# Maxima by half blocks, and eight weighing-only steps moved among the last groups of a graph attention kernel

## The chip, the core and the metric

The kernel runs on one core of a Trainium2 chip. The core has five engines with queues of their own: TensorE (PE; its weight loads are listed as PEld), VectorE (DVE), ScalarE (ACT), GpSimd (POOL) and SyncE (SP, which here only issues DMAs). The metric is the device time of one execution in microseconds; less is better. The median of several runs stands for a kernel.

## The reference

One layer of relational graph attention with residual and two layer norms, on 3125 nodes of 128 values and 100,000 edges, sorted by destination (about 32 edges to a node), each with one of 5 relations; 8 heads of 16.

```python
x_src, x_dst = node_embeddings[src], node_embeddings[dst]
for r in range(5):
    mask = edge_types == r
    q = jnp.einsum('eh,khd->ekd', x_dst, W_Q[r])
    k = jnp.einsum('eh,khd->ekd', x_src, W_K[r])
    v = jnp.einsum('eh,khd->ekd', x_src, W_V[r])
    logits = (q * k).sum(-1) / 4 + attn_bias[r][None, :]
    masked = jnp.where(mask[:, None], logits, -1e9)
    max_v = jax.ops.segment_max(masked, dst, num_segments=n)
    exp_l = jnp.where(mask[:, None], jnp.exp(masked - max_v[dst]), 0.0)
    sum_exp = jax.ops.segment_sum(exp_l, dst, num_segments=n)
    attn = exp_l / (sum_exp[dst] + 1e-12)
    out = out + jax.ops.segment_sum(attn[:, :, None] * v, dst, num_segments=n)
h = out.reshape(n, 128) @ out_proj_w.T + out_proj_b + node_embeddings
y = layernorm(h) * gamma + beta
result = layernorm(x + y)
```

So every edge needs the largest logit of its node, relation and head before its weight can be formed.

## The kernel before, in words

Edges are cut into 196 groups of 512 in the order of their destinations; nodes into 25 blocks of 128. A first phase (to about 135 us) makes a table `kv_d` of keys and values, one row for each node and relation, the first queries, and the place `start_i` in the edge list where each node begins, with its number of edges `deg`. `checks` counts nodes that have too many edges or begin too far from where an even spread would put them; if there is any, a general path is run in place of this one.

Then comes one loop over steps `k`, written out by hand: the order in which instructions are issued is the order on each engine. A step does the first half of the work for one group `g` and the second half for an earlier group `v`.

First half, group `g`: POOL gathers the group's 512 rows of `kv_d` with four indirect DMAs (`gather`, L618) into one of 24 buffers, in the loop up to three steps ahead (`AHEAD`, one step near the end). SP fetches `kt` (keys for the one-hot matrix `hot`) and `qw` (queries of the nodes in the group's window, L720) three steps ahead. PE spreads the queries over the edges (`spread_q`, L734), DVE multiplies and sums (`logits`, L747, L748), SP stores the logits with their relation to `lg_d` (L753).

Maxima, for each block `b` of 128 nodes, one node on a partition: when the last group that can hold an edge of the block has its logits (`full_at`, step `full_step[b]`), POOL loads 64 edges' logits for each node from `start_i` on (`maxima_load`, tile `ell`, L760). This load stands in POOL's queue behind the gathers issued so far and ahead of all later ones, and it waits for the stored logits. `maxima(b, c0, c1)` then runs in two steps, relations 0 to 2 and 3 to 4: ACT turns `ell` to head-major order (`by_head`, L772), DVE closes the edges of other relations (`shut`, L782), adds (L787) and reduces (L793), on 8 heads x 64 edges for each relation; six small operations split the result into three bfloat16 parts `m3`. SP stores them to `m_d` (`store_m`, L807) and fetches the rows of a window for each later group (`fetch_m`, tile `mw`, L815).

Second half, group `v`: PE spreads the maxima over the edges (`spread_m`, L825), DVE subtracts (`less_max`, L833), ACT takes the exponential (L837), DVE weighs the values (`weigh`, L842), ACT makes the one-hot matrix of places `at` (L862, L865; near the end DVE makes two of its four parts, L857), PE sums by node and relation (`sums`, L876; what belongs to a node cut by the group's edge is carried over, L878), DVE divides (`norm`, L897 to L900), PE adds the relations (L885), and ACT puts the result in its place (`by_node`, L910). A gather's buffer comes free when its group has been weighed.

For each block, when its groups are summed (`done_at`): projection (L917, L918), residual and moments (`residual`), square root on ACT (`roots`, L943, which needs another activation table than the exponential; a table load takes 1.28 us) and norms on DVE (`norms`, L948 to L968), store (L976). A block whose `root_at` would fall between the last group's first half and the last group's second half is put off to the end, so that the table is exchanged once.

The plan: `step_of[g]` is the step of the first half, `at_k[v]` that of the second half. `ready[b] = full_step[b] + lag(b)`, with a lag of 8 steps (7 for the last three blocks): load at `full_step + 1`, maxima at `ready - 5` and `ready - 4`, store at `ready - 3`, fetch from `ready - 2` on. Group `v` may not be weighed before `ready` of the block in which its last node can lie (`block_of`). `CATCH_UP` is a set of groups after each of which a step without a first half is put in; before, it is empty. So the first halves take steps 0 to 195, second halves lag 19 steps in the steady part, and 19 steps (196 to 214) hold only second halves: these are called weighing-only steps here. In them `spread_m` repeats its columns 16 times rather than 8 (only the first copy is used).

Of the kernel before, what the change touches and what calls it, by code (L numbers as in the profile page):

```python
# [17 lines left out]
P = 128  # L18
# [29 lines left out]
CATCH_UP = ()  # L48
# [6 lines left out]
LAG = 8  # L55
SR = 250
# [43 lines left out]
def slack(b):  # L100

    n = min(P * b, N)
    e = E * n / N
    return int(5.0 * max(e * (1 - e / E), 0.0) ** 0.5) + 16 if 0 < n < N else 0


def full_at(b, more=0):

    last = P * E // N * (b + 1) + slack(b + 1) + more
    return -(-min(E, last) // GE) - 1 if b < NT - 1 else NGR - 1  # L110


def block_of(g):

    return min(
        b for b in range(NT)
        if b == NT - 1 or P * E // N * (b + 1) - slack(b + 1) >= min(E, (g + 1) * GE)
    )


def windowed_path(
# [25 lines left out]
    start_i = keep("start_i", [P, NT], I32)  # L147
    deg = keep("deg", [P, NT])
# [126 lines left out]
    cap = load.tile([P, NT], F32, name="cap")  # L275
    for b in range(NT):
        nc.gpsimd.memset(off[:, b : b + 1], float(slack(b)))
        nc.gpsimd.memset(cap[:, b : b + 1], float((full_at(b, D) + 1) * GE - D))
# [194 lines left out]
    begin = load.tile([P, NT + 1], F32, name="begin")  # L473

    def starts():
# [5 lines left out]
        nc.vector.tensor_tensor(start_i, begin[:, :NT], cap, op=ALU.min)  # L481
# [3 lines left out]
        nc.vector.tensor_tensor(deg, endp, begin[:, :NT], op=ALU.subtract)  # L485

    def checks():
        many = load.tile([P, NT], F32, name="many")
        nc.vector.tensor_scalar(
            many, deg, float(D), None, op0=ALU.is_gt, op1=ALU.add, accum_out=vio[:, 3:4]  # L490
# [5 lines left out]
        nc.vector.tensor_tensor(dev[:, 0, :], dev[:, 0, :], off, op=ALU.is_gt)  # L496
        dsum = load.tile([1, 1], F32, name="dsum")
# [17 lines left out]
    def small():  # L515
        nc.vector.tensor_scalar_mul(bias4, bias4, 4.0)
        nc.vector.tensor_tensor(lift, lift, beta_t[0:1, :], op=ALU.subtract)
        op_ = pps.tile([P, P], F32, name="op_", tag="tr", bufs=2)
        nc.tensor.transpose(op_, ow, ident)
        nc.scalar.copy(out_wT, op_)  # L520
# [20 lines left out]
    def no_maxima():  # L541
# [26 lines left out]
        21: [checks],  # L568
# [189 lines left out]
    def maxima_load(b):  # L758
# [3 lines left out]
            in_=lg_d[: (full_at(b, D) + 1) * GE, :],  # L762
# [4 lines left out]
    def maxima(b, c0, c1):  # L767

        if c0 == 0:
            ell = live.pop(("ell", b))  # L770
            by_head = ps.tile([P, HEADS, D], F32, name="by_head", bufs=1)
            nc.scalar.copy(by_head, ell[:, :, :HEADS].rearrange("p s k -> p k s"))  # L772
# [4 lines left out]
            mx = late_flow.tile([P, R, HEADS], F32, name="mx", bufs=1)  # L777
            live["max", b] = by_head, mine, mx
        by_head, mine, mx = live["max", b]
        shut = late_flow.tile([P, RH, D], F32, name="shut", bufs=1)  # L780
        for r in range(c0, c1):
# [3 lines left out]
        wl = late_flow.tile([P, RH, HEADS, D], F32, name="wl", tag="wl", bufs=1)  # L785
        n = c1 - c0
        nc.vector.tensor_tensor(  # L787
            wl[:, :n],
            by_head[:, None].to_broadcast([P, n, HEADS, D]),
            shut[:, :n, None, :].to_broadcast([P, n, HEADS, D]),  # L790
            op=ALU.add,
        )
        nc.vector.tensor_reduce(mx[:, c0:c1], wl[:, :n], AX.X, ALU.max)  # L793
# [3 lines left out]
        nc.vector.tensor_tensor(mx, mx, bias4, op=ALU.add)  # L797
        nc.vector.scalar_tensor_tensor(mx, mx, NEG4, bias4, op0=ALU.max, op1=ALU.subtract)
        m3 = late_flow.tile([P, R, 3, HEADS], BF16, name="m3")
        nc.vector.tensor_copy(m3[:, :, 0, :], mx)  # L800
        nc.vector.tensor_tensor(mx, mx, m3[:, :, 0, :], op=ALU.subtract)
        nc.vector.tensor_copy(m3[:, :, 1, :], mx)
        nc.vector.tensor_tensor(m3[:, :, 2, :], mx, m3[:, :, 1, :], op=ALU.subtract)
        live["m3", b] = m3

    def store_m(b):
        nc.sync.dma_start(  # L807
            m_d[b * P * R : (b + 1) * P * R, :].rearrange("(p r) c -> p (r c)", r=R),
            live.pop(("m3", b)).rearrange("p r s k -> p (r s k)"),
        )  # L810

    def fetch_m(g):
        mw = late_flow.tile([P, 3, HEADS], BF16, name="mw", bufs=4)
        f = window(g, first5, SPE)
        nc.sync.dma_start(mw.rearrange("w s k -> w (s k)"), m_d[bass.ds(f, P), :])  # L815
        live["mw", g] = mw


    def spread_m(g, times):

        me = ps.tile([P, T, times, HEADS], F32, name="me", tag="me")
        hot, mw = live.pop(("hot", g)), live.pop(("mw", g))
        for t in range(T):
            for s in range(3):
                nc.tensor.matmul(  # L825
                    me[:, t], hot[:, t, :], mw[:WR, s, None, :].to_broadcast([WR, times, HEADS]),
                    start=(s == 0), stop=(s == 2),
                )
        live["mde", g] = me[:, :, 0, :]
# [156 lines left out]
    def lag(b):  # L986

        return LAG if b < NT - 3 else LAG - 1

    full_step = [step_of[full_at(b, D)] for b in range(NT)]  # L990
    ready = [full_step[b] + lag(b) for b in range(NT)]


    at_k, k = {}, 0
    for v in range(NGR):
        k = max(k + 1, ready[block_of(v)])
        at_k[v] = k
    v_at = {k: v for v, k in at_k.items()}
    last_k = at_k[NGR - 1]
    done_at = {b: at_k[full_at(b)] + 4 for b in range(NT)}  # L1000
# [26 lines left out]
    for k in range(-3, root_at[NT] + 2):  # L1027
# [8 lines left out]
        for b in range(NT):  # L1036
            if done_at[b] - 1 == k:
                fetch_x("xr", b)
            if norm_at[b + 1] + 1 == k:
                store_z(b)  # L1040
            if ready[b] - 3 == k:
# [3 lines left out]
        for u in range(NGR):  # L1045
            if max(at_k[u] - 3, ready[block_of(u)] - 2) == k:
# [8 lines left out]
        for b in range(NT):  # L1055
# [21 lines left out]
        if v_at.get(k + 1) is not None:  # L1077
            spread_m(v_at[k + 1], 8 if k + 1 in group_at else 16)
# [27 lines left out]
        for b in range(NT):  # L1106
            if ready[b] - 5 == k:
                maxima(b, 0, RH)
            if ready[b] - 4 == k:
                maxima(b, RH, R)  # L1110
# [525 lines left out]
```

## Time and profile before

| | |
|---|---|
| median of 9 runs | 1763.12 us (1741.0 to 1767.3) |
| profiled execution | 1753.77 us, its span 1751.8 us |
| granted TensorE clock, mean | 0.708 |
| busy: PE, PEld | 1022.2 us (58%), 771.9 us (44%) |
| busy: DVE, ACT, POOL | 947.6 (54%), 638.6 (36%), 797.9 us (46%) |
| first logits (L747) | 135.3 us |
| logits of groups 157, 192, 195 | 1386.6, 1655.9, 1673.9 us |
| weighing (L842) of groups 0, 183, 195 | 289.8, 1700.7, 1729.3 us |

Times inside an execution are counted from its first instruction. In a profile line of a timeline there stand start, duration, engine, line, operation, output and inputs with partitions x elements, how many, and in brackets how long the engine had been idle and what ended that. "issue" means that nothing in the profile explains the wait; "remote" that the releaser isn't known.

### The profile page before, as it was taken

What the parts mean: (1) busy time and instruction counts of PE and PEld (TensorE: products, weight loads), DVE (VectorE), ACT (ScalarE), POOL (GpSimd) and SP (SyncE); (2) the same over time, 40 slices, a digit from 0 to 9 for tenths busy, and PEclk for the clock granted to TensorE, in tenths of its full rate; (3) what the DMA queues carried; (4) which work ended last, traced back from release to release, by engine and by line L of the source; (5) the groups of instructions that cost most, each with busy time, mean ns of one, the idle gap of its engine ahead of it and who ended that gap; (6) DMA issues with size and microseconds to landing.
All of it is one profiled execution on the core that took longest, in us unless ns stands there. A gap on an engine that the chain in (4) does not pass through costs nothing.

```text
span 1751.8 us, 26103 instructions
## 1 busy us (share of the span) xinstructions
PE 1022.2 (58%) x7738; PEld 771.9 (44%) x7738; DVE 947.6 (54%) x2531; ACT 638.6 (36%) x2257; POOL 797.9 (46%) x904
## 2 busy tenths in 40 slices
PE   5773727256556646645664575566557556454776
PEld 2442525145345435534453454445345345343664
DVE  2551526265546655754565466556546546553786
ACT  0540103134334434433443353343335334342544
POOL 5507051634535555544545545454454544644300
PEclk7996867577666766866676666766677666666788
DMA  5764243344445445534544444454454444434310
GB/s 132 252 266 125 69 120 69 100 110 114 110 113 128 124 104 134 134 99 111 136 119 108 132 117 116 115 136 108 103 138 111 108 120 107 126 109 104 86 25 14
DMA packets 181508, 203.67 MB, mean 116 GB/s; under 512 B 83508, under 2 KB 146381, under 8 KB 181238
## 3 DMA queue, kind: packets, MB, share of 16 engines
q0 software_dynamic: 40672, 112.08, 22.4%
q1 hardware_dynamic: 136928, 86.33, 20.6%
q10 hardware_dynamic: 3758, 3.51, 0.8%
q8 instruction: 64, 1.05, 0.2%
q14 instruction: 86, 0.70, 0.1%
HBM read 166.51 MB, written 35.29 MB: 115 GB/s over the span
## 4 chain that ended last, share of the span: by engine, by line
DVE 28%; PE 25%; another core or an unknown queue 21%; issue 15%; ACT 6%; DMA 3%; SPq 1%; DVEq 0%; POOL 0%; ACTq 0%; POOLq 0%
PE pp L876 7%; PE me L825 4%; DVE wl L787 4%; DVE mx L793 4%; DVE prod L747 4%; PE qe L734 3%; DVE lg L748 3%; DVE wv L842 2%; PE pr L362 2%; ACT at L862 2%; PE pp L878 2%; DVE hot L725 2%; PE pk L701 1%; PE prq L644 1%
## 5 line engine op out<-in xcount | busy, mean ns | idle before, releaser
L618 POOL DMA_INDIRECT kv<-kv_d,idx x764 | 722.8, 946 | 537.9 <-DVE den L897 278.9
L876 PE MATMUL pp<-wv,at 128*125 128x136 f32 x1568 | 383.1, 373 | 92.6 <-issue 85.1
L876 PEld LDWEIGHTS pp<-wv,at 128*125 128x125 f32 x1568 | 285.8, 246 | 181.9 <-issue 167.0
L734 PE MATMUL qe<-qw,hot 125*128 125x128 bf16 x2352 | 230.6, 254 | 162.3 <-issue 127.6
L825 PE MATMUL me<-mw,hot 125*128 125x64 bf16 (+1 forms) x2352 | 146.4, 216 | 224.6 <-issue 120.8
L734 PEld LDWEIGHTS <-hot 125*128 125x128 bf16 x2352 | 198.3, 123 | 179.4 <-issue 148.9
L862 ACT ACTIVATE at<-row_at,nkey 128x125 f32<-128x125 f32 x744 | 237.6, 398 | 0.0
L825 PEld LDWEIGHTS <-hot 125*128 125x128 bf16 x2352 | 125.2, 112 | 250.4 <-issue 190.6
L833 DVE TENSOR_TENSOR me<-lg,me 128x32 f32<-128x32 f32 x196 | 37.6, 192 | 359.3 <-remote 267.0
L837 ACT ACTIVATE me<-me 128x32 f32<-128x32 f32 x196 | 35.7, 182 | 529.5 <-DVE me L833 447.5
L842 DVE TENSOR_TENSOR wv<-kv,me 128x512 f32<-128x512 f32 x196 | 132.9, 678 | 161.7 <-remote 103.9
L747 DVE TENSOR_TENSOR prod<-kv,qe 128x512 f32<-128x512 f32 x196 | 132.9, 678 | 83.7 <-remote 74.0
L760 POOL DMA_INDIRECT ell<-lg_d,start_i x25 | 23.6, 944 | 308.7 <-ACT me L837 79.0
L878 PE MATMUL pp<-pt,carried 125*5 125x136 f32 x390 | 97.0, 336 | 74.7 <-ACT pt L891 47.8
L748 DVE TENSOR_REDUCE lg<-prod 128x32 f32<-128x512 f32 x196 | 134.5, 686 | 6.8
L910 ACT COPY oT<-pp 128x25 f32 x196 | 33.6, 171 | 273.5 <-PE me L825 90.6
L865 ACT ACTIVATE at<-at 128x500 f32<-128x500 f32 (+1 forms) x196 | 117.3, 599 | 6.2
L644 PE MATMUL prq<-wq,xTq 128*128 128x384 f32 (+1 forms) x88 | 52.0, 687 | 89.1 <-DVE hot L725 72.9
L885 PEld LDWEIGHTS pp<-rsum,o 125*128 125x128 f32 x392 | 80.7, 248 | 16.8 <-issue 16.1
L787 DVE TENSOR_TENSOR wl<-by_head,shut 128x1536 f32<-128x1536 f32 (+1 forms) x50 | 74.5, 1491 | 14.4 <-PE pk L701 6.4
L885 PE MATMUL pp<-rsum,o 125*128 125x25 f32 x392 | 72.6, 265 | 13.2 <-issue 8.7
L793 DVE TENSOR_REDUCE mx<-wl 128x24 f32<-128x1536 f32 (+1 forms) x50 | 74.3, 1487 | 1.7
(182 smaller groups left out, 1179.8 us busy)
## 6 DMA issues: line engine op xcount, KB each, us to landing
kt<-key_d SPq DMA_DIRECT2D x196, 128.0 KB
qw<-q_d SPq DMA_DIRECT2D x196, 96.0 KB
kv_d<-kvs SPq DMA_DIRECT2D x24, 640.0 KB
kv<-kv_d,idx POOLq DMA_INDIRECT x764
q_d<-q SPq DMA_DIRECT2D x22, 480.0 KB
lg_d<-lg SPq DMA_DIRECT2D x196, 18.0 KB
mw<-m_d SPq DMA_DIRECT2D x196, 6.0 KB
xr<-in_x SPq DMA_DIRECT2D x24, 64.0 KB
```

The costliest lines, as they stand in the source:

```text
L618: nc.gpsimd.indirect_dma_start(out=kv[:, t, :], out_offset=None, in_=kv_d[:, :], in_offset=bass.IndirectOffsetOnAxis(ap=idx[:, t, g : g + ...
L734: nc.tensor.matmul(qe[:, t, :], hot[:, t, :], qw[:WR, s, :], start=(s == 0), stop=(s == 2))
L747: nc.vector.tensor_tensor(prod, kv[:, :, :H], live.pop(("qe", g)), op=ALU.mult)
L748: nc.vector.tensor_reduce(lg[:, :, :HEADS], prod.rearrange("p t (k d) -> p t k d", d=HD), AX.X, ALU.add)
L787: nc.vector.tensor_tensor(wl[:, :n], by_head[:, None].to_broadcast([P, n, HEADS, D]), shut[:, :n, None, :].to_broadcast([P, n, HEADS, D]), ...
L793: nc.vector.tensor_reduce(mx[:, c0:c1], wl[:, :n], AX.X, ALU.max)
L825: nc.tensor.matmul(me[:, t], hot[:, t, :], mw[:WR, s, None, :].to_broadcast([WR, times, HEADS]), start=(s == 0), stop=(s == 2),)
L842: nc.vector.tensor_tensor(wv[:, :, :H].rearrange("p t (k d) -> p t k d", d=HD), kv[:, :, H:].rearrange("p t (k d) -> p t k d", d=HD), live ...
L862: nc.scalar.activation(at[:, t, :], row_at[:, :WR], AF.Abs, bias=nkey[:, t, g : g + 1], scale=1.0)
L876: nc.tensor.matmul(pp, at[:, t, :], wv[:, t, :], start=(t == 0), stop=(t == T - 1))
L878: nc.tensor.matmul(pp[:R], carried[:WR, g, :], live.pop(("pt", g - 1)), start=False, stop=False,)
L885: nc.tensor.matmul(op, live.pop(("o5", done)), rsum[:WR], start=True, stop=True)
```

## The change

Three things change together.

1. The last six blocks (19 to 24) have their maxima made by halves of 64 nodes: `MB` now lists 30 parts, 19 whole blocks and 11 halves (the 25th block has 53 nodes, so one half). For a half, the 64 nodes stand on both sets of 64 partitions; the lower set works on heads 0 to 3, the upper on heads 4 to 7. So one pass has 5 relations x 4 heads x 64 edges, and `maxima` runs in one step. Each half has its own `ell` load, `deg` and `start_i` columns (made in the first phase by `halves`), its own `bias_h`, and two stores. `checks` looks at the half-block starts too. The lag is 6 steps for a half (`LAG_H`).
2. `CATCH_UP` gets eight groups: after each of 163, 167, ... 191 a weighing-only step is put in. First halves take steps 0 to 203, second halves end at step 214 as before, and 11 weighing-only steps are left after the last first half. The lag of the second half falls from 19 to 11 steps over the last 33 groups.
3. The layout of `m_d`, `m3` and `mw` is now half the heads, part, head; and a weighing-only step repeats its columns 12 times, not 16.

In the plan blocks 20 and 21 now have their roots at steps 194 and 201; before, both stood behind the last weighing step.

```diff
-CATCH_UP = ()
+CATCH_UP = (163, 167, 171, 175, 179, 183, 187, 191)
...
+LAG_H = 6
+HALVED = 5
...
+NF = NT - 1 - HALVED
+MB = [(P * b, P * (b + 1), None) for b in range(NF)]
+for b in range(NF, NT):
+    MB += [(n, min(n + P // 2, N), b) for n in range(P * b, min(P * (b + 1), N), P // 2)]
+MEND = tuple(n for _, n, _ in MB)
+NM = len(MB)
...
+    def halves():
+
+        hp = pps.tile([P, 2, 2, NT - NF], F32, name="hp", tag="tr", bufs=2)
+        for h in range(2):
+            twice = load.tile([P, 2, P // 2], F32, name=f"twice{h}")
+            nc.vector.tensor_copy(
+                twice, ident[:, None, h * P // 2 : (h + 1) * P // 2].to_broadcast([P, 2, P // 2])
+            )
+            for i, a in enumerate((begin[:, NF:NT], degs[:, NF:])):
+                nc.tensor.matmul(
+                    hp[:, i, h, :], twice.rearrange("p a b -> p (a b)"), a, 
+                    start=h == i == 0, stop=h == i == 1,
+                )
...
         if c0 == 0:
             ell = live.pop(("ell", b))
-            by_head = ps.tile([P, HEADS, D], F32, name="by_head", bufs=1)
-            nc.scalar.copy(by_head, ell[:, :, :HEADS].rearrange("p s k -> p k s"))
+            by_head = ps.tile([P, HEADS, D], F32, name="by_head", bufs=1)[:, :nh]
+            if whole:
+                nc.scalar.copy(by_head, ell[:, :, :HEADS].rearrange("p s k -> p k s"))
+            else:
+                for h in range(2):
+                    at = slice(h * P // 2, (h + 1) * P // 2)
+                    nc.scalar.copy(
+                        by_head[at], ell[at, :, h * nh : (h + 1) * nh].rearrange("p s k -> p k s")
+                    )
...
         nc.vector.tensor_tensor(
-            wl[:, :n],
-            by_head[:, None].to_broadcast([P, n, HEADS, D]),
-            shut[:, :n, None, :].to_broadcast([P, n, HEADS, D]),
+            wl,
+            by_head[:, None].to_broadcast([P, n, nh, D]),
+            shut[:, :n, None, :].to_broadcast([P, n, nh, D]),
             op=ALU.add,
         )
-        nc.vector.tensor_reduce(mx[:, c0:c1], wl[:, :n], AX.X, ALU.max)
+        nc.vector.tensor_reduce(mx[:, c0:c1], wl, AX.X, ALU.max)
...
     def store_m(b):
-        nc.sync.dma_start(
-            m_d[b * P * R : (b + 1) * P * R, :].rearrange("(p r) c -> p (r c)", r=R),
-            live.pop(("m3", b)).rearrange("p r s k -> p (r s k)"),
-        )
+        n0, n1, part = MB[b]
+        m3 = live.pop(("m3", b))
+        to = m_d[n0 * R : (n0 + (P if part is None else P // 2)) * R, :]
+        if part is None:
+            nc.sync.dma_start(
+                to.rearrange("(p r) c -> p (r c)", r=R), m3.rearrange("p r h s k -> p (r h s k)")
+            )
+        else:
+            to = to.rearrange("(p r) (h c) -> h p r c", r=R, h=2)
+            for h in range(2):
+                nc.sync.dma_start(
+                    to[h],
+                    m3[h * P // 2 : (h + 1) * P // 2, :, 0].rearrange("p r s k -> p r (s k)"),
+                )
...
-        return LAG if b < NT - 3 else LAG - 1
+        return LAG if MB[b][2] is None else LAG_H
 
-    full_step = [step_of[full_at(b, D)] for b in range(NT)]
-    ready = [full_step[b] + lag(b) for b in range(NT)]
+    full_step = [step_of[full_at(n, D)] for n in MEND]
+    ready = [full_step[b] + lag(b) for b in range(NM)]
...
-            spread_m(v_at[k + 1], 8 if k + 1 in group_at else 16)
+            spread_m(v_at[k + 1], 8 if k + 1 in group_at else 12)
...
-            if ready[b] - 5 == k:
+        for b in range(NM):
+            whole = MB[b][2] is None
+            if ready[b] - 5 == k and whole:
                 maxima(b, 0, RH)
             if ready[b] - 4 == k:
-                maxima(b, RH, R)
+                maxima(b, RH if whole else 0, R)
```

The last groups of the parts from block 18 on have their logits at steps 153, 157, 161, 166, 171, 176, 181, 185, 190, 195, 200 and 203; before, those of blocks 18 to 24 at 153, 161, 169, 177, 184, 192 and 195. Weighing-only steps stand at 164, 169, 174, 179, 184, 189, 194, 199 and 204 to 214.

## The prediction

> **What bounds the kernel now.** I read the share of each engine first (PE 58%, DVE 54%, POOL 46%: none is full), then the waits of POOL between the logits of group 163 and the last logits, since there the stretch that the change rewrites lies.
>
> ```profile
> POOL kv L618 <- DVE den L897: 40.8, 9, 10.2
> POOL ell L760 <- ACT lg L741: 26.8, 2, 13.4
> POOL ell L760 <- DMA lg_d<-lg: 14.4, 1, 14.4
> POOL ell L760 <- DMA mw<-m_d: 13.6, 1, 13.6
> ```
>
> Columns: total us, times, longest. POOL waits for kv buffers to come free (weighing holds them) and 13.4 to 14.4 us at each load of `ell`, because that load needs the logits of its block's last group and POOL has by then gathered three steps ahead. After it POOL runs without a pause (timeline of POOL, one gather each 1.25 us: 0.95 and 0.30 idle):
>
> ```profile
> 1483.87 0.95 POOL L760 DMA_INDIRECT ell<-lg_d,start_i  x1 [13.40 <-ACT lg L741]
> 1485.12 0.95 POOL L618 DMA_INDIRECT kv<-kv_d,idx  x1 [0.30 <-issue]
> ...
> 1498.88 0.94 POOL L618 DMA_INDIRECT kv<-kv_d,idx  x1 [0.30 <-issue]
> 1503.44 0.94 POOL L618 DMA_INDIRECT kv<-kv_d,idx  x1 [3.62 <-DVE den L897]
> ```
>
> In such a burst the other engines almost stop. Same place, stretches of a window query (us, then busy time of PE, PEld, DVE, ACT, POOL, granted clock, DMA share, GB/s), and the logits on DVE:
>
> ```profile
> 1473.80:1483.80 10.00, 8.13 (x68) 6.53 (x66) 7.87 (x24) 5.30 (x22) 0.00 (x0) 0.59 0.28 47
> 1483.80:1489.00 5.20, 4.25 (x54) 3.45 (x52) 2.32 (x6) 4.74 (x10) 3.92 (x5) 1.00 0.76 220
> 1489.00:1502.50 13.50, 1.63 (x13) 1.09 (x14) 3.72 (x15) 2.19 (x9) 8.38 (x9) 0.62 0.52 137
> ```
>
> ```profile
> 1480.14 0.68 DVE L747 TENSOR_TENSOR prod<-kv,qe 128x512 f32<-128x512 f32 x1
> 1483.81 0.68 DVE L747 TENSOR_TENSOR prod<-kv,qe 128x512 f32<-128x512 f32 x1
> 1493.20 0.20 DVE L833 TENSOR_TENSOR me<-lg,me 128x32 f32<-128x32 f32 x1 [7.05 <-remote]
> 1493.94 0.68 DVE L747 TENSOR_TENSOR prod<-kv,qe 128x512 f32<-128x512 f32 x1
> 1503.82 0.68 DVE L747 TENSOR_TENSOR prod<-kv,qe 128x512 f32<-128x512 f32 x1
> ```
>
> 54 matmuls in the first 5.2 us of the burst, 13 in the next 13.5 us. The step that follows comes 4.0 us after the burst's end (1499.8 to 1503.8). What holds PE back I can't see in these rows (the DMA share is 0.52); I use only that it happens: in the middle of the run too, a burst of 17 (982.5 to 1003.6) lets 52 matmuls through in its first 5.5 us and 17 in the next 15.0. So main steps cost POOL's burst plus what is left of the steps when it has ended, and the kernel is bound by this alternation. At the end it is otherwise: POOL is idle, and the weighing-only steps follow one another.
>
> ```profile
> 1673.90:1700.70 26.80, 19.85 (x151) 16.70 (x149) 24.62 (x78) 11.23 (x46) 0.94 (x1) 0.76 0.09 20
> 1700.70:1729.30 28.60, 28.60 (x294) 23.95 (x292) 22.87 (x91) 19.72 (x85) 0.00 (x0) 1.00 0.04 6
> 1729.30:1751.80 22.50, 6.03 (x36) 4.11 (x35) 12.44 (x54) 4.49 (x15) 0.00 (x0) 0.69 0.08 24
> ```
>
> From the last logits (1673.9) to the first group of the last block weighed (183, at 1700.7): the way through `ell`, maxima, store and fetch. Then 12 more steps of 2.38 us, PE 28.6 of 28.6 busy. Then 22.5 us of projection and norms.
>
> **The end, which gets shorter.** The plan has 227 steps before and after; eight weighing-only steps go from the end into the main part (19 become 11).
> - Six groups (190 to 195) instead of 13 depend on the last part: seven steps fewer at 2.38 = -16.7 us.
> - Maxima of the last part. DVE, by shape:
>
> ```profile
> L787 DVE TENSOR_TENSOR wl<-by_head,shut 128x1536 f32<-128x1536 f32 x25 | 43.9, 1758 | 7.2 <-ACT by_head L772 5.6 <-DVE shut L782 0.7 <-issue 0.3
> L793 DVE TENSOR_REDUCE mx<-wl 128x24 f32<-128x1536 f32 x25 | 43.8, 1753 | 0.9
> L787 DVE TENSOR_TENSOR wl<-by_head,shut 128x1024 f32<-128x1024 f32 x25 | 30.6, 1224 | 7.2 <-PE pk L701 6.4
> L793 DVE TENSOR_REDUCE mx<-wl 128x16 f32<-128x1024 f32 x25 | 30.5, 1220 | 0.9
> ```
>
> A whole block: 1.76 + 1.75 + 1.22 + 1.22, `mine` 0.33, `shut` 0.7, six small ones 1.4 = 8.4 us. A half has 20 x 64 = 1280 elements, midway: 1.49 + 1.49 + 0.33 + 0.7 + 1.4 = 5.4. With the weighing that lay between the two stages (1.7 us), -4.5 on this way; the store is now two DMAs of 24-byte pieces, 0 to +1 us (an estimate: 423 packets of SP's queue around 1006 us took 25 ns each in the mean, and each of 16 engines gets 20 of the 320 pieces): -4.
> - Blocks 20 and 21 are normed in the main part. In the last 22.5 us two of six rounds go, each about 1.7 us (DVE 1738.6 to 1740.4): -3.5, of which the main part pays up to two exchanges of ACT's table, 2 x 2 x 1.28 = 5, if nothing hides them; ACT idles in bursts, I take 0.
> - `times` 12 for 16: 96 for 128 columns in 12 matmuls, 0.83 to 0.67 us, x 6 = -1.
>
> Sum of the end: -16.7 - 4 - 3.5 - 1 = -25 us, bounds -20 and -28.
>
> **The main part, which gets longer.** Logits 157 to 192 take 1386.6 to 1655.9 = 269.3 us before. In POOL's order there now stand, between one `ell` and the next from block 18's load on, 16, 12, 16, 16, 16, 16, 12, 12, 16, 16 gathers where there were 32. Each next `ell` again needs logits that POOL has long passed, and the buffers bind no more, because weighing runs closer behind (19 steps fall to 11): so all gathers between two loads run as one burst. An interval, from logits of the last group of one part to those of the next:
> - logits to `ell`: 1480.1 to 1483.9 = 3.8 us;
> - burst of 17: 17 x 1.25 = 21.2 (of 13: 16.2);
> - burst's end to the third step's main work: 4.0;
> - the fourth and fifth step, one weighing-only. The nearest rows are the two steps after a burst with POOL silent: logits 1473.8, 1480.1, 1483.8 = 6.3 + 3.7; the weighing-only one lacks logits and `qe` (1.4 on DVE): about 8.
>
> So 37 us with 16 gathers; 32 with 12 (185 to 190); 28 with 12 and only four steps (181 to 185); 29 for 157 to 161, which has none alone. Sum: 29 + 4 x 37 + 28 + 32 + 2 x 37 = 311, +42 us. The 5.4 us of half maxima lie under the burst here: `ell` lands 6.3 us after issue (1677.6 to 1683.9) while DVE idles in the crawl. If that cover is gone, each interval gets up to 5.5 more (by_head and chain after the burst).
> Lower bound of an interval: the four steps from 1473.8 to 1503.8 took 30.0 us with a burst of 13; add only a bare weighing step, 2.3: 32.3, the other gathers and maxima hidden. Upper: 30 + 2.3 + 4 x 1.25 + 5.5 = 42.8. I take 37, which is also built from the nearest burst of 17. The last three groups keep their 18 us.
>
> The other queues that the moved steps pass: on SP a weighing-only step issues one `mw` fetch (0.34 us and a register load of 0.27), and eleven halves store twice where six blocks stored once, 16 more x 0.35 = 5.6 us over 311. Behind a store that waits for `m3` stand `kt` and `qw` of three steps ahead, so it takes from that lead first: 0. On ACT a half's two copies (64 partitions x 256 each) cost between 2 x 0.28 (the 136-element copy) and 1.06 (the whole one): under the burst as well.
>
> The PE clock decides part of the 8 us. A weighing-only step's PE work takes 0.83 + 0.91 + 0.40 + 0.50 + 0.30 = 2.9 us at clock 1.00 (step at 1722.2) and 1.44 + 1.67 + 0.62 + 0.82 + 0.46 = 5.0 at half (step at 1673.8). The Trainium skill, "TensorE: Matmul & The Clock Gate", section "What's actually happening", says the array falls to half rate after an idle window of about 3.4 us and needs as long a busy one to come back; it speaks against weighing steps placed behind bursts, and the granted 0.59 in the stretch above agrees. By it the 8 us stand; by the end's row at full clock they would be 6, the sum 16 us less.
>
> Early work: the new small operations in the table phase (`halves`, more `checks`, 11 POOL memsets of 0.23) are about 3 us on DVE and 2.5 on POOL, under the table matmuls: 0, at most +3. The strided `mw` reads have as many columns: 0.
>
> **Sum.** +42 - 25 = +17 on the span 1751.8 (execution 1753.77). The median of the runs, 1763.12, lies 9.4 us above that execution; I put the difference on the median: 1780, and 1782 with half of the early work and table exchanges.
>
> **Rivals.**
> 1. Hidden: alone steps, extra loads and half maxima fit into POOL's 13-us waits. Intervals at 32.3, the three short ones at 27, 25 and 27 (157 to 161 took 26.9 before): 6 x 32.3 + 79 = 273, +4; less 25 = -21: 1742. For it: none of the engines is full. Against: in those waits the steps run that POOL waits for.
> 2. Slower yet: maxima fall behind the burst, as they did for block 22 (burst of 21 from 1592, the next less-max only at 1620.4, then maxima). They then delay the fetch of `mw`, on which the less-max ahead of the next logits waits. Intervals 42.8 (37.8, 33.8, 34): 34 + 6 x 42.8 + 33.8 + 37.8 = 362, +93 - 25 = +68: 1831. It decides from intervals of 40 on. For it: the store now comes two steps after the load. Against: in bursts of 13 two steps still got through.
> 3. The start checks (now at half blocks too) reject the input and the general path runs: over twice the time. Same slack rule as before, so 1%.
>
> **How the numbers follow.** Likeliest (37 us intervals, own range 1762 to 1805) 0.50; hidden 0.27; slower yet 0.22; general path 0.01. Break-even is an interval of some 35 (17 us over nine intervals are 1.9 each). The range takes both rivals: 1740 to 1832. What a measurement here can tell from no change is 0.5%, 1754 to 1772: faster 0.26, same 0.17 (the lower edge of the likeliest, the upper of the hidden), slower 0.57.
>
> **What would show it.** In the profile after: unbroken bursts of 13 or 17 after the loads of the halves, with PE crawling from about 6 us on; logits 157 to 192 in about 311 us; last logits to end 53 us instead of 77.9. Wrong if bursts are broken up, if PE doesn't crawl in them, or if intervals are at 31 or below.

## The result, and the profile after

The changed kernel takes 8394.79 us (median of 20 runs, 8363.43 to 8419.89) against 1759.77 us for the kernel before (62 runs, 1732.91 to 1775.71): ratio 4.795, interval 4.785 to 4.805. The forecast of 1782 us missed by a factor of 4.7. The time splits in two, as a table of stretches of the kernel after shows (from : to and length in us, then busy time and instructions of PE, PEld, DVE, ACT, POOL, the granted clock, the DMA share and GB/s):

```profile
0.00:1768.00 1768.00, 1008.98 (x7746) 764.82 (x7746) 956.50 (x2601) 658.58 (x2294) 807.77 (x925) 0.71 0.45 117
1768.00:8395.50 6627.50, 592.99 (x2153) 404.24 (x2153) 2642.04 (x6072) 69.00 (x152) 3350.97 (x3255) 0.51 0.13 39
```

The first 1768 us hold the whole windowed path: 7746 matmuls, where the kernel before had 7738 in all. What follows is another program. The timeline of the kernel after shows where it begins (start, length, engine, line, what is written):

```profile
1758.90 0.93 SPq L1063 DMA_DIRECT2D out<-z  x2
1759.03 0.20 POOL masks.py:197 MEMSET ident<- 128x128 f32 x1 [42.38 <-ACT sd L1030]
1759.21 0.34 DVE L1055 TENSOR_SCALAR z<-y,mv,sd 53x128 f32<-53x128 f32 x1
1759.57 0.85 ACTq L1281 DMA_DIRECT2D x_t<-in_x  x1
```

While the last rows `z` of the finished output are still being written, POOL builds an identity matrix again and ACT's queue loads `x` into `x_t`: lines from 1224 on are `general_path`, the version for inputs that the windows don't fit. It runs behind the windowed path, not in its place. Among the costliest groups of the kernel after are four gathers or scatters of 782 pieces each, none of them in the profile before:

```profile
L1322 POOL DMA_INDIRECT by_pair<-pay,pos_i x782 | 822.7, 1052 | 1107.7 <-DVE pos_i L1354 858.6
L1322 POOL DMA_INDIRECT presorted<-pay,pos_i x782 | 759.6, 971 | 1153.0 <-DVE pay L1312 914.7
L1482 POOL DMA_INDIRECT q<-q_tab,idx x782 | 895.9, 1146 | 544.8 <-issue 231.4
...
L1482 POOL DMA_INDIRECT kv<-kv_tab,idx x782 | 749.6, 959 | 288.0 <-issue 237.5
```

So `n_bad` was above zero at the branch (L95 to L97), and the answer was computed twice.

**Why the input is rejected.** The new part of `checks` compares the starts of the half blocks with their expected place for b = 19 to 24, all at once (`begin[half, NF:NT]`). Block 24 has 53 nodes, so its second half would begin at node 3136, past the last node 3124. Worked out from the code: every edge lies before that node, so its start is 100000; expected is 4096 x 24 + 2048 = 100352; the deviation is 352. `slack` cuts its argument at N and returns 0 there. 352 > 0 counts as one violation, for every input, because no number in it depends on the data. The second halves of blocks 19 to 23 deviate by 14 to 83 edges (worked out from the reference's input) with slacks of 316 to 649.

**The stretch that the change was about** can be read in the same trace. Logits of groups 157 and 192 in the kernel after (timeline of DVE):

```profile
1386.53 0.68 DVE L807 TENSOR_TENSOR prod<-kv,qe 128x512 f32<-128x512 f32 x1
...
1694.11 0.68 DVE L807 TENSOR_TENSOR prod<-kv,qe 128x512 f32<-128x512 f32 x1
```

307.6 us instead of 269.3. POOL in this stretch, waits by total, times and longest, and one burst out of its timeline:

```profile
POOL kv L678 <- issue: 37.8, 124, 0.3
POOL ell L820 <- ACT lg L801: 30.4, 2, 16.9
POOL ell L820 <- ACT wv L937: 16.8, 1, 16.8
POOL ell L820 <- DVE den L984: 15.9, 1, 15.9
```

```profile
1491.37 0.95 POOL L820 DMA_INDIRECT ell<-lg_d,start_i  x1 [15.72 <-DVE z L1055]
1492.62 0.95 POOL L678 DMA_INDIRECT kv<-kv_d,idx  x1 [0.31 <-issue]
...
1511.43 0.95 POOL L678 DMA_INDIRECT kv<-kv_d,idx  x1 [0.30 <-issue]
```

The waits for free `kv` buffers (`den`) that led the list before are gone. Every longer wait now stands at a load of `ell`, 13.5 to 16.9 us each, and then come the load and 12 or 16 gathers without a break; the burst shown has 16 and takes 21 us.

### The profile page after: what moved, and what is told of

Same layout as the page of the kernel before. It is cut to its first block, busy times and chain, and to the rows that moved or that the text cites. A ratio compares the mean times of both kernels' runs of the same rounds, so it can differ in the third digit from the quotient of the medians.

```text
span 8395.5 us, 54178 instructions
## 1 busy us (share of the span) xinstructions
PE 1602.0 (19%) x9899; PEld 1169.1 (14%) x9899; DVE 3598.5 (43%) x8673; ACT 727.6 (9%) x2446; POOL 4158.7 (50%) x4180
## 5 line engine op out<-in xcount | busy, mean ns | idle before, releaser
L1322 POOL DMA_INDIRECT by_pair<-pay,pos_i x782 | 822.7, 1052 | 1107.7 <-DVE pos_i L1354 858.6
L1322 POOL DMA_INDIRECT presorted<-pay,pos_i x782 | 759.6, 971 | 1153.0 <-DVE pay L1312 914.7
L1482 POOL DMA_INDIRECT q<-q_tab,idx x782 | 895.9, 1146 | 544.8 <-issue 231.4
L1542 DVE TENSOR_TENSOR_SCAN st<-ex,st 128x34 f32<-128x34 f32 x3128 | 651.0, 270 | 702.4 <-issue 696.5
L1482 POOL DMA_INDIRECT kv<-kv_tab,idx x782 | 749.6, 959 | 288.0 <-issue 237.5
L1345 DVE TENSOR_TENSOR_SCAN run<-ones_c,here 128x782 f32<-128x782 f32 x254 | 453.9, 1787 | 8.8
L1433 DVE TENSOR_TENSOR hot<-lane,digits 128x4352 bf16<-128x4352 bf16 x46 | 212.3, 4686 | 412.6 <-remote 343.0
L1350 DVE SCALAR_TENSOR_TENSOR run<-run,off,here 128x782 f32<-128x782 f32 x254 | 262.4, 1033 | 9.1
L1407 PE MATMUL pr<-w,xT 128*128 128x512 f32 x200 | 176.4, 1015 | 400.5 <-issue 280.4
L1351 DVE TENSOR_TENSOR pos<-pos,run 128x782 f32<-128x782 f32 x254 | 247.4, 974 | 0.0
```

Of the source, the lines that this page charges most:

```text
L1322: st = nc.gpsimd.indirect_dma_start(out=table[:, :], out_offset=bass.IndirectOffsetOnAxis(ap=pos_i[:, j : j + 1], axis=0), in_=pay[:, j, : ...
L1345: nc.vector.tensor_tensor_scan(run, ones_c, here, 0.0, op0=ALU.mult, op1=ALU.add)
L1350: nc.vector.scalar_tensor_tensor(run, run, off, here, op0=ALU.add, op1=ALU.mult)
L1351: nc.vector.tensor_tensor(pos, pos, run, op=ALU.add)
L1407: nc.tensor.matmul(pr[:, : b1 - b0, :], xT, w[:, b0:b1, :], start=True, stop=True)
L1433: nc.vector.tensor_tensor(hot[:, s], lane[:, None, :].to_broadcast([P, J, P]), digits[:, s, g * J : (g + 1) * J, None].to_broadcast([P, J, ...
```

## The experiments

Runs that were sent together share a chip and its runs of the kernel before. The ratios are against those. "The main part" is the time from the logits of group 157 to those of 192, read in the trace; "the end" is from the last logits (group 195) to the end of the span.

### The check without the half that isn't there

```
-        devh = load.tile([P, 2, NT - NF], F32, name="devh")
+        devh = load.tile([P, 2, NT - 1 - NF], F32, name="devh")
-            dh[:, 0, :], begin[half, NF:NT], ..., mid[half, NF:],
+            dh[:, 0, :], begin[half, NF : NT - 1], ..., mid[half, NF : NT - 1],
-        ... off_h[half, NF:], op=ALU.is_gt)
+        ... off_h[half, NF : NT - 1], op=ALU.is_gt)
```

> The changed kernel with its new test of half-block starts left off for block 24, whose half would begin at node 3136 of 3125. Theory A (that node counts as displaced: its start is the end of the list, 100000, where 100352 is expected, and the allowance there is 0; so the general path runs after the windowed one): the general path is gone and the span is the windowed part of the changed kernel, whose last norm ended at 1759.5 us against 1746.2 before, so about 1765, ratio to before about 1.005 to 1.01. Rival B (another of the tests trips as well, the node degrees or the other starts): still about 8390 us. Rival C (the time is lost in the windowed part): between 1800 and 8390.

1793.47 us against 1778.02: ratio 1.0081, interval 1.0045 to 1.0117, as theory A has it. The general path is gone with this one edit, so the missing half of block 24 was the whole cause of the factor. From here on "the mended kernel" is this one. What is left is what the prediction had priced: +14 us. Main part 310.4 us (1413.6 to 1724.0), end 55.6 us (1741.3 to 1796.9).

### The kernel before, rejected

```
-        nc.gpsimd.memset(off[:, b : b + 1], float(slack(b)))
+        nc.gpsimd.memset(off[:, b : b + 1], float(slack(b) if b < NT - 1 else -400))
```

> The kernel before, with an allowance of -400 for block 24's start, so that its test rejects the input although the starts are good. Theory A: 1752 + (8395.5 - 1759.5) = about 8388 us, since the general path alone is the difference. Rival C (the changed kernel loses time elsewhere too): below 8330.

8400.25 us in a single run, close to the 8388 of theory A. The stretches of this run, cut at the same places:

```profile
0.00:1768.00 1768.00, 1018.27 (x7734) 767.33 (x7734) 942.14 (x2510) 636.89 (x2253) 798.86 (x904) 0.71 0.45 115
1768.00:8398.00 6630.00, 595.49 (x2157) 405.76 (x2157) 2653.32 (x6108) 70.23 (x157) 3357.65 (x3260) 0.51 0.14 39
```

Old code with a count above zero: 6630 us behind the cut, where the changed kernel had 6627.5. Neither the half maxima nor the moved steps make any of it.

### Halves alone

The mended kernel with `CATCH_UP = ()`.

> The mended kernel with CATCH_UP empty: halves, but all 19 weighing-only steps at the end. Theory M (each load of a part starts a burst in which the other engines crawl, so that five more loads lengthen the main part, and weighing-only steps among the groups cost about 4 us each): logits 157 to 195 take 295 to 315 us instead of 287, the end stays near 73 us, span 1755 to 1775. Rival H (the weighing-only steps are hidden in POOL's waits, so moving them is a gain of some 17 us): e3 is slower than the mended kernel by 10 us or more.

1799.97 us, ratio 1.0106 (1.0070 to 1.0142). Main part 292.2, end 75.2 (before 269.3 and 77.9). The logits of groups 157 to 195 take 309.6 us, within the 295 to 315 of theory M. The median is 6.5 us above that of the mended kernel, with intervals that overlap, so rival H (10 us or more) isn't met. The five added loads of `ell` (30 in all instead of 25) and what they bring with them cost some 23 us, and the end gains 2.7 us, as the order of the weighing stays as it was. Against it the mended kernel has 18.2 us more in the main part and 19.6 less at the end: a moved step costs 2.3 us and saves 2.45.

### Steps alone

The kernel before with `CATCH_UP = (163, 167, 171, 175, 179, 183, 187, 191)`, whole blocks throughout.

> Before, with the eight added steps and whole blocks throughout. Without halves the last block is ready seven steps after the last logits as before, so the plan has 232 steps instead of 227, of which 16 (before 19) come after the last main step. Theory E (a moved step costs in the main part about what it saves at the end, 2.3 us, and the extra loads of ell cost the rest): logits 157 to 192 rise from 269 by 8 x 2.3 to about 288, the end falls from 78 by three steps to about 71, the ratio is 1.005 to 1.010. Rival L (the steps cost little by themselves and it is their meeting with the halves' loads that costs): 157 to 192 below 278, the ratio 1.00 or under.

1797.4 us against 1762.2: ratio 1.0242 (1.0159 to 1.0326). Both expectations missed. The end is as worked out (70.2 us), but the main part is 321.9 us, longer than with the halves. POOL's waits for free buffers in the main part, before and in this run, and its timeline and the stretches of one interval of this run say why:

```profile
POOL kv L618 <- DVE den L897: 56.0, 12, 10.2
POOL kv L618 <- DVE den L897: 25.2, 5, 12.8
```

```profile
1637.22 0.94 POOL L760 DMA_INDIRECT ell<-lg_d,start_i  x1 [36.28 <-ACT me L837]
```

```profile
1637.20:1641.20 4.00, 4.00 (x52) 3.25 (x51) 2.53 (x6) 2.14 (x9) 3.07 (x4) 1.00 0.47 113
1641.20:1679.00 37.80, 5.59 (x28) 3.48 (x26) 7.14 (x13) 3.46 (x11) 28.12 (x30) 0.57 0.41 118
```

A block is now up to ten steps long. POOL waits 36.3 us at this load, and then issues 33 (the load and 32 gathers) in one burst, 41 us, in which PE gets through 80 matmuls. The kernel before has as many gathers between two loads, but there waits for free buffers break them up, so that its bursts in this stretch have at most 21 pieces; here, with the weighing closer behind, the four bursts that a load begins have 21 to 33. Halves and moved steps belong together: the halves cut down the bursts that the steps leave unbroken (at most 17 in the mended kernel). Neither theory had these longer bursts.

### No late gathers

The mended kernel, in which the gathers of groups 161 to 195 are left out (so these groups compute with older rows).

```
-        if g in XG:
+        if g in XG or g > 160:
             return
```

> The mended kernel without the gathers of groups 161 to 195 (left out: these groups' keys and values; stale rows stand in their buffers). Theory M (bursts of gathers hold PE back and set the intervals of 37 us): logits 157 to 192 take under 230 us instead of 307.6, no stretch with PE at one matmul per us. Rival L (the chain load, maxima, store, fetch sets the interval): they stay above 290 us. In between: both share it.

Main part 208.2 us instead of 310.4 (whole kernel 1688.06 us, a single run), under the 230 of theory M. A third of the stretch is due to its gathers.

### Plain loads in their place

The mended kernel; groups 161 to 195 load 128 consecutive rows of the table instead of gathered ones.

```
+            if g > 160:
+                nc.gpsimd.dma_start(kv[:, t, :], kv_d[(g % 64) * P : (g % 64 + 1) * P, :])
+                continue
```

> The mended kernel with the gathers of groups 161 to 195 replaced by plain loads of 128 consecutive rows from the same queue of GpSimd, of the same size, so that the output is another. Theory I (the indirect issue by GpSimd is what starves TensorE, not the bytes): logits 157 to 192 near the 208 us of the kernel without late gathers, at most 235. Rival D (the bytes moved and the queue's packets do it): 157 to 192 stays above 280.

Main part 214.3 us, under the 235 of theory I. The same stretch of work in three kernels, in this order: the mended one, without late gathers, with plain loads:

```profile
1413.60:1724.00 310.40, 161.20 (x1479) 129.76 (x1477) 177.88 (x529) 134.50 (x471) 133.64 (x141) 0.69 0.43 102
```

```profile
1391.00:1599.00 208.00, 151.83 (x1449) 123.19 (x1450) 172.44 (x509) 129.68 (x458) 11.36 (x13) 0.79 0.31 69
```

```profile
1386.60:1600.90 214.30, 150.48 (x1480) 122.49 (x1478) 176.58 (x529) 133.13 (x471) 79.45 (x141) 0.82 0.56 146
```

The number of matmuls and PE's busy time are about the same in all three; only the time in between differs. With the plain loads the stretch moves its bytes at 146 GB/s, more than the 102 with gathers, and PE isn't held up. So neither the bytes nor the place of the transfers in POOL's program is enough to make the crawl. What in the indirect form does isn't separated, because more than the form changes: the rows are consecutive, POOL needs about 0.53 us for one load instead of 0.95, and the burst shown here falls into two short runs:

```profile
1464.38 3.76 POOL L679 DMA_DIRECT2D kv<-kv_d  x7
1472.07 4.76 POOL L679 DMA_DIRECT2D kv<-kv_d  x9 [3.93 <-issue]
```

In the bursts of gathers the crawl begins 2 to 7 us after the load and lasts to their end, so runs as short as these might not show it.

### Breaks between late gathers

The mended kernel with two tiny memsets on POOL behind each gather of groups 161 to 195.

```
+            if g > 160:
+                for _ in range(2):
+                    nc.gpsimd.memset(pause, 0.0)
```

> The mended kernel with two memsets of one element on GpSimd behind each gather of groups 161 to 195, which widen the pitch of a burst from 1.25 to about 2.2 us. Theory R (it is the density of gathers that starves TensorE, and at a wider pitch it keeps working): the crawl in bursts goes, intervals of 37 us fall to about 36 or less though 16 gathers now take 35 us, and the ratio to before stays at or below 1.01. Rival B (TensorE is held back for as long as GpSimd issues gathers, whatever their pitch): intervals grow by about 16 x 0.95 = 15 us to 50, and the ratio goes to 1.05 or more.

1764.46 us against 1762.2: ratio 1.0051 (1.0009 to 1.0093), which overlaps that of the mended kernel without breaks. Main part 295.6 us, 15 less than in the mended kernel's trace (nearly the same program took 307.6 in the kernel after, so two traces of it differ by 3). The pitch (from one gather to the next) grew less than meant, as POOL's timeline shows, because the memsets fill the 0.30 us in which POOL idled before:

```profile
1497.26 0.95 POOL L679 DMA_INDIRECT kv<-kv_d,idx  x1
1498.21 0.24 POOL L685 MEMSET pause<- 1x1 f32 x2
1498.60 0.95 POOL L679 DMA_INDIRECT kv<-kv_d,idx  x1
```

1.33 us a gather, with a longer break after every fourth; a burst of 17 takes 22 to 24 us instead of 21. The rival's 50 us were for a pitch of 2.2 us, so this run doesn't test it; at this pitch it would add some 2 us to an interval, where the main part got shorter. That breaks help was still a reading of one trace.

### Half maxima for the last block only

The kernel after with `HALVED = 1`, `CATCH_UP = ()`, no test of half starts and the old lags of whole blocks: only the last block of 53 nodes takes the new form, with no added load.

> Before, with the half form of the maxima for the last block of 53 nodes alone (one part, no added load of ell, no moved steps, no test of half starts). By the terms of the prediction the main part stays as it is (269 us on a chip at the level of the first profile) and the end loses the 4 us of smaller maxima and about 1 us of the narrower times, so the ratio is 0.995 to 1.000; if half maxima save nothing on the way to the last block's weighing, 1.000 or above.

1766.36 us, ratio 1.0036 (0.9990 to 1.0083): no gain is shown, and a small loss is open. The end stays at 77.6 us (before 77.9). The stage itself is shorter, 5.6 us from `mine` to `m3` (1700.89 to 1706.46) for the 10.8 us of before with a weighing between (1683.60 to 1694.36). SP's queue shows where a part goes; the store of the maxima and the next fetches, before and in this run:

```profile
1694.38 0.35 SPq L807 DMA_DIRECT2D m_d<-m  x1
...
1696.05 4.59 SPq L815 DMA_DIRECT2D mw<-m_d  x5
```

```profile
1706.49 1.21 SPq L882 DMA_DIRECT2D m_d<-m  x2
1709.84 11.38 SPq L890 DMA_DIRECT2D mw<-m_d  x7
```

From the store's issue to the first fetch 1.67 us with one store, 3.35 us with the two stores of a half. The rest goes to steps that stand in the plan ahead of the first group of the last block: its weighing, at 1720.3, comes 10.5 us behind the fetch, where it came 4.7 us behind it. The granted clock goes with that. The maxima and the way from there to that weighing, before and then in this run:

```profile
1683.60:1694.40 10.80, 7.96 (x59) 6.31 (x58) 9.77 (x25) 3.33 (x11) 0.00 (x0) 0.86 0.04 8
1694.40:1700.70 6.30, 4.89 (x51) 4.24 (x51) 5.90 (x26) 4.25 (x19) 0.00 (x0) 1.00 0.09 11
```

```profile
1700.90:1706.50 5.60, 1.62 (x6) 1.04 (x6) 5.01 (x15) 1.49 (x4) 0.00 (x0) 0.61 0.01 1
1706.50:1720.30 13.80, 12.76 (x79) 10.63 (x80) 7.89 (x33) 6.21 (x26) 0.00 (x0) 0.54 0.07 6
```

Before, a weighing lay between the two parts of the maxima, PE was busy for 7.96 of 10.80 us, and the steps behind them ran at the full clock. Made in one step, the maxima leave PE busy for 1.62 of 5.60 us, and the steps behind them run at 0.54.

### Breaks behind every gather, on two chips

The kernel before, and the mended one, with the two memsets behind the gathers of all groups; then the kernel before with six.

> Before, with two memsets of one element on GpSimd behind each gather of every group (in the late groups of the mended kernel they took 15 of 310 us off logits 157 to 192, though the pitch only rose from 1.25 to 1.33 us and more). If breaks between gathers feed TensorE in bursts wherever they come, each interval of eight steps in the main part (63 us, with bursts of 13 to 17) loses 2 to 4 us, over 20 intervals 40 to 80 us: ratio 0.955 to 0.98. Rival: the intervals of before are set by the steps and the waits for free buffers, not by the crawl, and bursts of one load in eight steps leave room for it: ratio 0.995 to 1.01.

> The mended kernel with the same two memsets behind the gathers of every group. If breaks help in every burst: the late part as in the run with late breaks (157 to 192 about 296) and the middle 40 to 80 us less, ratio to before 0.96 to 0.985, and against before with breaks still 0 to 10 us slower, because six more loads of ell are six more bursts. Rival as above: the ratio stays at 1.00 to 1.01.

> Before with six memsets instead of two behind each gather, which widen the pitch to about 1.9 us. If the width of the break counts (TensorE gets its instructions while GpSimd issues none), this is faster than with two, ratio 0.94 to 0.97, until GpSimd itself becomes the bound: 784 gathers at 1.9 are 1490 us, close to the 1540 of the main part. If only the presence of a break counts, it equals the kernel with two breaks; if GpSimd becomes the bound, ratio above 1.02.

1361.73, 1369.18 and 1800.97 us, ratios 1.1162 (1.1114 to 1.1209), 1.1222 (1.1175 to 1.1270) and 1.4759 (1.4696 to 1.4822). The expectations of the first two don't hold; of the third's, the branch in which GpSimd becomes the bound (above 1.02) does. For on this chip the kernel before took 1219.73 us in the median (7 runs, 1216.59 to 1227.30), 540 to 560 us less than on the others. Here the breaks cost what they take: the memsets of two are busy for 140.4 us, and the time grew by 142.0. With six, POOL's pitch is 1.9 us or more, which for 764 gathers makes 1450 us; that it sets the time is likely, but not shown further. The mended kernel stays behind the one before by a half per cent (1369.18 / 1361.73 = 1.0055, both with breaks). The exchange is much the same here, though PE doesn't crawl in these bursts: main part 231.5 us against 205.4, end 53.2 against 78.8.

> Before with two memsets behind each gather, once more, because on the chip of the last three runs the kernel before took 1220 us and not 1760. There GpSimd was the bound and the 140 us that the memsets are busy came on top (1362). On a chip where before takes about 1760 us and TensorE starves in bursts: if breaks feed TensorE, ratio 0.955 to 0.98; if the two late traces differed by chance and breaks do nothing there, 0.995 to 1.01; if GpSimd's longer bursts only add to the intervals, 1.02 to 1.08. On a chip where before takes about 1220 us: 1.116 again, and nothing new of the crawl.

The first of the three once more, and on a chip where the kernel before takes 1778.54 us: 1726.59 us, ratio 0.9730 (0.9684 to 0.9777), as expected if breaks feed TensorE. There it has the lowest ratio of the kernels here that compute the whole result; on the chip of 1220 us the same file is 11.6% slower than the kernel it comes from. Where it gains isn't what was expected: logits of the first to those of group 40 take 311.0 us (before 350.0, and 349 to 351 in every other trace without early breaks on the slower chips). From there to group 157 it needs 920.5 (before 901.3); kernels whose program for these groups is nearly that of the kernel before took 894 to 925 us, so neither a gain nor a loss shows in that stretch. The main part takes 267.2 (before 269.3). No trace of the kernel before was taken on this chip, and the two spans differ by only 27 us where the medians differ by 52.

Stretches within bursts, from some 6 us after the load of `ell` on: the kernel before, this run, and the same file on the chip of 1220 us:

```profile
988.50:1003.60 15.10, 3.95 (x15) 2.45 (x15) 1.11 (x4) 0.48 (x3) 11.44 (x13) 0.50 0.42 117
```

```profile
963.80:987.40 23.60, 10.30 (x54) 6.28 (x53) 7.39 (x17) 3.88 (x14) 18.45 (x50) 0.54 0.46 117
```

```profile
807.10:837.00 29.90, 21.31 (x196) 16.79 (x196) 24.16 (x66) 14.41 (x59) 22.79 (x63) 0.78 0.60 141
```

15 matmuls in 15.1 us without breaks, 54 in 23.6 us with them, 196 in 29.9 us on the other chip with the same breaks: 1.0, 2.3 and 6.6 per us. Over all bursts of 17 pieces or more, counted from 6.5 us behind the first piece to the last gather, the three traces give 0.6 to 1.6, 1.9 to 4.8 and 5.6 to 6.4 per us. Breaks feed PE, but no gain shows in the middle of the run, where the bursts also become longer with them. They pay in the first blocks, where a burst can have 33 pieces (the kernel before, then this run, load to load):

```profile
300.00:373.00 73.00, 30.75 (x253) 24.29 (x252) 30.53 (x77) 18.31 (x72) 31.20 (x33) 0.65 0.40 100
```

```profile
287.00:346.00 59.00, 29.74 (x246) 22.40 (x245) 30.17 (x74) 17.80 (x68) 37.29 (x98) 0.67 0.48 122
```

About as much PE work in 14 us less.

## Why the prediction failed, and what of it held

**The step that failed** is rival 3: "The start checks (now at half blocks too) reject the input and the general path runs: over twice the time. Same slack rule as before, so 1%." The mechanism was named and its time was on the right side, but it was put at next to nothing, and the sum at 1782 us rests on the general path not running. Its chance was given by analogy with the old check, which never looks past the last node. It could have been settled on paper: the check covers b = 19 to 24, the last block has 53 nodes, and for a half start at 3136 the slack is 0 and the deviation 352. A branch whose price is about 6630 us and whose condition can be worked out from the code doesn't get a chance but an answer. The runs showed that this condition alone decides (without it, ratio 1.0081; with the old code and a forced count, 8400 us).

**Main part, +42 us (311).** Measured 307.6 in the kernel after and 310.4 in the mended one. The intervals from the last logits of one part to those of the next, in the mended kernel: 29.5 (157 to 161), 35.3, 37.1, 36.1, 38.5, 29.1 (177 to 180), 30.6, 37.4, 36.9. The 37 us built from a burst of 17, and the shorter ones of 28 to 32, hold within 2 us each. The terms hold as well: in the six long intervals the load comes 3.7 to 5.1 us after the logits (3.8 predicted), the burst takes 20.9 to 21.1 us (21.2), and from its end to the next logits it is 9.2 to 13.8 us, 11.9 in the mean (4.0 + 8). That last term spreads more than the sum misses, so an agreement within 1 us of the 311 is partly luck. The half maxima lie under the burst, as predicted: in all nine intervals their additions (`wl`) begin and end within it. Rival 2 (42.8) and rival 1 (32.3) are both out. The steps behind a burst were priced at the lower clock, and the mended kernel shows it, in a burst from 6 us on and then behind it:

```profile
1525.00:1540.00 15.00, 2.31 (x18) 1.98 (x17) 7.22 (x21) 3.17 (x9) 11.34 (x13) 0.50 0.54 129
1540.00:1552.00 12.00, 8.30 (x76) 6.93 (x77) 6.39 (x21) 6.29 (x28) 0.12 (x1) 0.63 0.22 56
```

The granted clock is 0.50 in the crawl and 0.63 behind it, 0.69 over the main part of the mended kernel, and 0.79 and 0.82 in the two kernels without late gathers or with plain loads. This agrees with the Trainium skill, "TensorE: Matmul & The Clock Gate", section "What's actually happening", by which an idle array drops to half rate.

**End, -25 us (53).** Measured 55.6, so -22.3. By its terms: first weighing of the last part to its last, 28.6 to 11.8 us, -16.8 (predicted -17.7 with `times`). Projection and norms, 22.5 to 19.5, -3.0 (predicted -3.5). Last logits to the first weighing of the last part, 26.8 to 24.3, -2.5 (predicted -4). The last is mis-sized, and SP's queue in the mended kernel shows the term:

```profile
1755.50 1.22 SPq L893 DMA_DIRECT2D m_d<-m  x2
...
1758.92 4.13 SPq L901 DMA_DIRECT2D mw<-m_d  x5
```

3.4 us from store to fetch instead of 1.67: two stores of short pieces cost 1.7 us more, not "0 to +1". From the fetch to the weighing it is 6.65 us instead of 4.67, a change that the prediction put at nothing: the granted clock is 0.58 between 1755.4 and 1765.6, where it was 1.00 before, as in the run with the last block only. Against that the maxima stage gave 5.2 us (10.8 to 5.6, 1749.89 to 1755.47), and it began 1.1 us sooner after the last logits.

**The sum without the general path.** +17 on the span was forecast; 310.4 - 269.3 = 41.1 and 55.6 - 77.9 = -22.3 make +18.8, between traces from two groups of runs, and the runs give +14 (8 to 21 by the interval). The forecast was that of a kernel with another check.

**What the prediction left open** was what holds PE back in a burst. It isn't the bytes alone and it isn't the queue's place (plain loads, 214 us). It isn't a wait for another engine or a transfer that the profile shows: PE's waits in the kernel before, from 988.5 to 1003.6 us, all end with "issue" (total, times, longest), 10.3 of its 11.2 idle us:

```profile
PE qe L734 <- issue: 3.8, 3, 1.7
PE pp L876 <- issue: 3.4, 4, 1.1
PE pp L878 <- issue: 2.1, 2, 1.5
PE pp L885 <- issue: 1.0, 1, 1.0
```

Nor is it POOL's busy time alone: with two memsets behind each gather POOL is as busy in a burst (18.45 of 23.6 us against 11.44 of 15.1), and PE gets through twice as many matmuls per us.

## What to carry to other kernels

A check that guards a slow path is part of the kernel's time: when a change adds a test to it, work the test out for the last, ragged piece, and for every piece that doesn't exist, before anything else is priced. Moving steps ahead from the end only exchanged them about one for one here (2.3 for 2.45 us), because the main part had no free place for them, and finer pieces have to pay for what each of them adds, here a load on which a queue stands and a burst behind it. A shorter stage can also be paid for with the clock: in the trace where PE had less to do meanwhile, the steps behind it ran at a granted 0.54 instead of 1.00. A gain from breaking up such bursts was 2.7% on one chip and a loss of 11.6% on another, so measure it on the chips that will run it.

## What the runs showed of the hardware

- On the chips where the kernel before takes about 1760 us or more, TensorE runs on for 2 to 7 us in an unbroken burst of indirect gathers on POOL (in the kernel before mostly 42 to 51 matmuls with as many weight loads) and then gets through about one matmul per us, until 1 to 5 us after the last gather. Plain loads of more GB/s from the same queue, in shorter runs, don't do this (214 against 310 us for the same work; 208 with no late gathers at all).
- A pair of one-element memsets behind each gather (a pitch of 1.33 us, with a longer break after every fourth, for 1.25) raises that to 2.3 matmuls per us in the burst shown, 1.9 to 4.8 in all.
- The kernel before took 1760 to 1779 us in four groups of runs (their medians) and 1220 us on one chip, where PE gets 6.6 matmuls per us through a burst with such breaks. No trace of the kernel before without breaks was taken on that chip, and what differs between the chips isn't known; nor is what an indirect gather takes away from PE elsewhere.
- A stretch in which TensorE is mostly idle is followed by steps at a lower granted clock: busy for 1.62 of 5.60 us, then 0.54 over 13.8 us; busy for 7.96 of 10.80 us, then 1.00.
